# Turned tokens go to their partitions by 4 transfers of 256 KB per group in place of 16 of 64 KB; the turns read features with a step of 4

## The chip, the cores and the metric

The kernel runs on one core of a Trainium2 chip. The metric is the device time of one execution in microseconds. Before the change the median of three runs is 577.77 us (577.75 to 578.08). One further execution was taken with the hardware profiler; all rows quoted below come from it.

The core has a matrix engine (TensorE, in the rows PE; its weight loads have rows of their own, PEld), a vector engine (VectorE, DVE), an activation engine (ScalarE, ACT), a general engine (GpSimd, POOL) and a sync engine (SP) that here only issues transfers. ACT issues some transfers too. Each engine takes its own instructions strictly in order; engines wait for one another by semaphores. Data lies in a memory of 128 partitions (SBUF); products are summed in banks of a second one (PSUM).

## The reference

A conditioned block over x of 2 x 2048 x 512 (f32):

```python
emb = jnp.dot(silu(t), ada_w) + ada_b
shift_msa, scale_msa, gate_msa, shift_mlp, scale_mlp, gate_mlp = jnp.split(emb, 6, axis=-1)
norm = _ln(x) * (1.0 + scale_msa[:, None]) + shift_msa[:, None]
h = gelu(jnp.dot(norm, ssm_w1) + ssm_b1, approximate=False)
x = x + gate_msa[:, None] * (jnp.dot(h, ssm_w2) + ssm_b2)
norm2 = _ln(x) * (1.0 + scale_mlp[:, None]) + shift_mlp[:, None]
hf = gelu(jnp.dot(norm2, ff_w1) + ff_b1, approximate=True)
x = x + gate_mlp[:, None] * (jnp.dot(hf, ff_w2) + ff_b2)
```

`_ln` takes mean and variance over the 512 features. The first two matrices are 512 x 512, the third is 512 x 1024, the fourth 1024 x 512.

## The kernel before

The 4096 tokens are cut into 8 blocks of 512. In a block, partition p holds the four tokens 4p to 4p+3 as four rows c of 512 features. Each block passes through four matrix products, called in the rows by their outputs: hA (first layer), oA (second, added to x), hC (third), oC (fourth, added to x). A matrix product is cut into quarters and done by seven products of quarters, P1 to P7, in place of eight; the sums of quarters that this needs are made on DVE and POOL, and the seven results are added up partly in PSUM and partly by DVE (lines 831 to 851, 886, 934, 1001, 1052, 1098, 1151). The third layer of blocks 1 to 7 goes further: 26 products over a list of registers (`HK_P`), with sums on POOL (L1206) and reads of PSUM by ACT (L1297) and DVE (L1300). Before a product may begin again in a PSUM bank, the DVE or ACT read of what stood there must be over; so a late DVE read can hold PE up.

The order of the work on each engine is written out by hand. A pass over a product takes a table `hooks`: after product "P5", or after round "1b" of a cut product, or after step 17 of the 26, the operations hung there are issued. So an operation of the norm of a later block stands at a fixed place between the DVE reads of the product that PE is busy with.

The change lies in `Norm`. A norm makes statistics (L602, L603, L655 to L704), normalizes four rows c (`normal`, L719 on ACT), and must then turn the block, since a product needs features on the partitions and tokens along them. The turn goes in two steps:

- `turn(c)`, L730: DVE's STREAM_TRANSPOSE turns all 32 x 32 squares of row c, 128 x 512 numbers, from `nT` (or `x`, where the norm is made in place) into the tile `blocks`. There is one buffer of `blocks`.
- `move`, L739: transfers carry the turned squares to the partitions where they belong, back into `nT`. `Q` is 32 and `C` is 4. For each a (source partitions 32a to 32a+31) and each m (destination partitions 32m to 32m+31) there is one transfer of 32 partitions x 2 KB, 16 for a block's norm. With two engines in `engs`, even m go to SP and odd m to ACT.

Then `moved` (`modulate`, L767 on ACT, L769 on DVE) scales and shifts each feature by the block's conditioning, and sums and products follow.

A block's two norms are called `n1[i]` (before hA) and `n2[i]` (before hC). Block 0's first norm is turned by PE (L746). The other 15 use `turn` and `move`: 60 turns and 240 transfers. The turns of `n1[1]`, `n2[0]`, `n1[2]` and `n2[1]` hang in the passes of the first two blocks' hA, oA and hC, before 93 us. The turns of `n1[3]` to `n1[7]` and of `n2[7]` hang in the passes of the 26 products (L1300 between them); the turns of `n2[2]` to `n2[6]` hang in the passes of oC (`residual_in_leaves`, L1052; `residual_in_all_leaves`, L1151). Moves of `n1[1]` and of `n2[2]` to `n2[6]` use SP and ACT; the rest use SP alone, but for `n2[0]`, whose m = 0, 1 are issued by SP in the pass of hA of block 1 and m = 2, 3 by ACT behind that pass.

Of the kernel before, what the change touches and what calls it, by code (L numbers as in the profile page):

```python
# [140 lines left out]
def kernel(  # L141
# [16 lines left out]
    nc = tc.nc  # L158
# [3 lines left out]
    KD = D // P  # L162
    KH = H // P
    C = 4
# [34 lines left out]
    def load_x(i, pieces=1):  # L199
        xs[i] = big_tile(f"x_{i}")  # L200
        for s in range(pieces):
            c = slice(s * C // pieces, (s + 1) * C // pieces)
            nc.sync.dma_start(out=xs[i][:, c, :], in_=x_blk[i][:, c, :])
# [22 lines left out]
    def load_row(t, row):  # L226
        nc.sync.dma_start(out=t, in_=row.unsqueeze(0).to_broadcast([P, D]))
        return t
# [130 lines left out]
    def store_gates(g):  # L359

        to = gates_dram[g].rearrange("b (n m q) -> m b n q", n=KD, q=G)
        for m in range(P // G):
            rows_m = gate_rows[g][m * G : m * G + B, :].rearrange("p (n q) -> p n q", n=KD)
            nc.sync.dma_start(out=to[m], in_=rows_m)

    def load_gate(g, b):

        t = work.tile([P, D], F32, tag=f"gb{g}", name=f"gsb_{g}_{b}", bufs=1)
        gate_rows[g, b] = load_row(t, gates_dram[g][b])
# [143 lines left out]
    Q = P // C  # L513
# [69 lines left out]
    def hook(hooks, places, ops):  # L583

        for n, op in enumerate(ops):
            hooks.setdefault(places[min(n, len(places) - 1)], []).append(op)


    class Norm:
# [136 lines left out]
        def turn(self, c):  # L726

            if c == 0:
                self.bl = self.blocks()
            nc.vector.transpose(  # L730
                self.bl[:, :, :, c, :].rearrange("p m k q -> p k m q"),
                self.nT[:, c, :].rearrange("p (k m q) -> p k m q", k=KD, m=C),
            )

        def move(self, engs=(nc.sync,), part=range(C)):

            for a in range(C):
                for m in part:
                    engs[m % len(engs)].dma_start(  # L739
                        out=self.nT[m * Q : (m + 1) * Q, a, :],  # L740
                        in_=self.bl[a * Q : (a + 1) * Q, m].rearrange("p k c q -> p (k c q)"),
                    )

        def transpose(self, c, pts, first):
            for k in range(KD):
# [713 lines left out]
    hooks = {}  # L1459
# [21 lines left out]
    hooks = {}  # L1481
# [7 lines left out]
    n2 = {0: Norm(0, 2)}  # L1489
# [20 lines left out]
    hooks = {}  # L1510
# [4 lines left out]
    hook(hooks, ("P5", "P7"), fw1_sums[1:3])  # L1515
    hook(hooks, ("P6",), [lambda: gate_rows_of(5)])
    hook(hooks, ("P6", "P7", "P7", "P7"), [lambda c=c: n2[0].turn(c) for c in range(C)])
    hook(hooks, ("P7",), [lambda: n2[0].move((nc.sync,), (0, 1)), lambda: store_gates(5), lambda: load_gate(5, 0), lambda: store_gates(2)])
    load_x(2)
    hA[1] = First(1, n1[1].ops, hooks, FIRST)  # L1520

    n2[0].move((nc.scalar,), (2, 3))
    hA_sums = hA[1].summed(nc.vector)
    run(hA_sums[:2])
    n1[2] = Norm(2, 1)
# [1 line left out]
    hooks = {}  # L1529
# [14 lines left out]
    hooks = {}  # L1544
# [25 lines left out]
    hooks = {}  # L1570
# [10 lines left out]
    hooks = {}  # L1581
# [7 lines left out]
    hooks = {}  # L1589
# [28 lines left out]
    for i in range(1, NBLK):  # L1618
# [4 lines left out]
        hooks = {}  # L1623
        if i == 1:
            assert not fa_sums
        if i == 1:
            engs = dict.fromkeys(("P23", "P4"), nc.gpsimd) | dict.fromkeys(("P5", "P7", "P1", "P6"), nc.vector)
# [60 lines left out]
        hooks = {}  # L1688
        hC_sums = hC.summed(1, nc.vector if alone else nc.gpsimd)
        hook(hooks, EARLY, hC_sums)  # L1690
        engs = (nc.vector if alone else nc.gpsimd, nc.gpsimd, nc.gpsimd)
# [13 lines left out]
        if nx2:  # L1705
# [26 lines left out]
            if ahead:  # L1732
                hooks = {}
# [10 lines left out]
        hooks = {}  # L1744
# [107 lines left out]
        hooks = {}  # L1852
# [81 lines left out]
```

## Time and profile before

| | us |
|---|---|
| median of three runs | 577.77 |
| the profiled execution | 577.74 |
| its span, first to last instruction | 575.9 |
| PE busy | 570.8 (3443 instructions) |
| DVE busy | 453.6 (963) |
| POOL busy | 436.7 (460) |
| ACT busy | 292.7 (574) |

The granted TensorE clock is 1.0 over the execution. A row of the waits reads: engine, tile and line that waited, what ended the wait, sum in us, times, longest. A row of the groups reads: line, engine, operation, out<-in, shapes, count, then busy us and mean ns of one, then idle time of the engine just before them and what ended most of it. A row of the timeline reads: start us, length us (from the first start to the last end where xN instructions are merged), engine, line, operation, and in brackets the idle time before it. PEld stands for the weight load with which a matmul begins; where a matmul must wait, its weight load waits.

### The profile page before, as it was taken

How to read it: one execution, taken by the hardware profiler on the slowest of the kernel's cores; microseconds unless marked ns; L12 is line 12 of the kernel's file. 1: busy time of each engine (PE TensorE's matmuls, PEld its weight loads, DVE VectorE, ACT ScalarE, POOL GpSimd, SP SyncE). 2: the span in 40 equal slices, each digit the busy share in tenths (PEclk: the TensorE clock that was granted, in tenths of full speed). 3: DMA queues.
4: the chain of work that ended last, by engine and by line, in shares of the span. 5: the costliest groups of instructions: out<-in, count | busy, mean ns of one | idle time of the engine just before them, and what ended most of it. 6: DMA issues, size and time to landing. Idle time of an engine off the chain costs nothing.

```text
span 575.9 us, 10119 instructions
## 1 busy us (share of the span) xinstructions
PE 570.8 (99%) x3443; PEld 514.1 (89%) x3443; DVE 453.6 (79%) x963; ACT 292.7 (51%) x574; POOL 436.7 (76%) x460
## 2 busy tenths in 40 slices
PE   8999999999999999999999999999999999999997
PEld 4888888888899889998899988998889999899897
DVE  4968898996878586987869877996768598897676
ACT  3727457705652875448734588326655431742430
POOL 1665449999949869889898999998994885379361
PEclk9999999999999999999999999999999999999999
DMA  8977333303205223283032930243240240031002
GB/s 329 390 232 249 100 71 92 96 38 146 58 18 162 106 100 69 97 260 126 1 93 50 330 115 21 54 109 122 101 109 2 110 126 23 1 73 74 2 1 73
DMA packets 26863, 62.30 MB, mean 108 GB/s; under 512 B 5136, under 2 KB 6204, under 8 KB 25148
## 3 DMA queue, kind: packets, MB, share of 16 engines
q1 hardware_dynamic: 22784, 55.87, 29.9%
q10 hardware_dynamic: 4028, 5.79, 3.9%
q8 instruction: 27, 0.44, 0.4%
q14 instruction: 24, 0.20, 0.1%
HBM read 35.94 MB, written 9.97 MB: 80 GB/s over the span
## 4 chain that ended last, share of the span: by engine, by line
PE 97%; DMA 2%; SPq 0%; DVE 0%; issue 0%; DVEq 0%
PE px_hC L1283 11%; PE py_hA L565 10%; PE py_hC L1283 8%; PE pv_hC L1283 8%; PE pl_oC_P_y L1038 5%; PE py_oC L990 5%; PE pv_hA L565 5%; PE py_oA L925 5%; PE pl_oC_A_y L1133 4%; PE py_oA L565 4%; PE pl_oC_P_v L1038 3%; PE pl_oC_B_y L1133 3%; PE py_hC L565 2%; PE px_hA L565 2%; PE py_oC L565 2%; PE pl_oA_y L940 2%
## 5 line engine op out<-in xcount | busy, mean ns | idle before, releaser
L656 POOL TENSOR_TENSOR r<-ve,minus_half 128x4 f32<-128x4 f32 x16 | 16.6, 1037 | 57.7 <-DVE ve L655 50.7
L767 ACT ACTIVATE nT<-nT,mod,mod 128x512 f32<-128x512 f32 x32 | 23.4, 803 | 46.2 <-DMA nT<-blocks 16.3
L1206 POOL TENSOR_TENSOR forms<-forms 128x256 f32<-128x256 f32 x56 | 42.5, 759 | 3.8 <-DVE forms L1202 0.4
L1283 PE MATMUL py_hC<-forms,fw 128*128 128x256 f32 x168 | 40.9, 379 | 0.0
L1300 DVE TENSOR_TENSOR hClo<-hClo,py_hC 128x512 f32<-128x512 f32 x42 | 28.5, 683 | 11.6 <-ACT hClo L1297 8.2
L719 ACT ACTIVATE nT<-x,nmr,rstd 128x512 f32<-128x512 f32 x36 | 26.8, 803 | 19.4 <-DVE nmr L704 16.8
L1283 PEld LDWEIGHTS py_hC<-forms,fw 128*128 128x128 f32 x168 | 31.7, 190 | 4.6 <-DVE hClo L1300 0.2
L386 POOL TENSOR_TENSOR hSC<-hClo,hChi 128x512 f32<-128x512 f32 (+1 forms) x16 | 19.2, 1205 | 18.7 <-ACT hChi L1278 17.9
L602 DVE BATCH_NORM_STATS2 st<-x 128x6 f32<-128x512 f32 x42 | 28.4, 675 | 4.9 <-DMA x<-in_x_dram 4.9
L1300 DVE TENSOR_TENSOR hChi<-hChi,pv_hC 128x512 f32<-128x512 f32 x35 | 23.2, 678 | 9.2 <-PE pv_hC L1283 5.0
L1278 ACT ACTIVATE hClo<-hClo,colsT 128x256 f32<-128x256 f32 x56 | 25.3, 498 | 5.0 <-DVE hClo L1300 4.8
L1283 PE MATMUL px_hC<-forms,fw 128*128 128x256 f32 x112 | 27.6, 379 | 0.0
L767 ACT ACTIVATE x<-x,mod 128x512 f32<-128x512 f32 x24 | 17.5, 801 | 18.8 <-DMA x<-blocks 18.8
L386 POOL TENSOR_TENSOR hClo<-hClo 128x512 f32<-128x512 f32 (+1 forms) x23 | 26.5, 1154 | 0.0
L1278 ACT ACTIVATE hChi<-hChi,colsT 128x256 f32<-128x256 f32 x56 | 25.1, 496 | 1.9 <-DVE hChi L1300 1.9
L730 DVE STREAM_TRANSPOSE blocks<-nT 128x512 f32<-128x512 f32 x36 | 24.2, 695 | 1.7 <-ACT nT L719 1.7
L1297 ACT ACTIVATE hChi<-py_hC 128x512 f32<-128x512 f32 x14 | 7.6, 594 | 34.0 <-PE py_hC L1283 14.8
L1297 ACT ACTIVATE hClo<-px_hC 128x512 f32<-128x512 f32 x21 | 12.5, 596 | 22.5 <-PE px_hC L1283 18.9
L1283 PEld LDWEIGHTS px_hC<-forms,fw 128*128 128x128 f32 x112 | 21.3, 190 | 2.9
L565 PE MATMUL py_hA<-x,w 128*128 128x256 f32 x96 | 22.7, 379 | 0.0
L1300 DVE TENSOR_TENSOR hChi<-hChi,px_hC 128x512 f32<-128x512 f32 x28 | 19.1, 682 | 4.3 <-ACT hClo L1297 2.1
L1283 PE MATMUL px_hC<-forms,fw_s 128*128 128x256 f32 x84 | 20.5, 380 | 0.0
(537 smaller groups left out, 1921.9 us busy)
## 6 DMA issues: line engine op xcount, KB each, us to landing
x<-in_x_dram SPq DMA_DIRECT2D x13, 1024.0 KB
out_dram<-x SPq DMA_DIRECT2D x14, 512.0 KB
x<-blocks SPq DMA_DIRECT2D x96, 64.0 KB
nT<-blocks SPq DMA_DIRECT2D x88, 64.0 KB
ada<-in_L_cond_ada_w_dram SPq DMA_DIRECT2D x5, 1024.0 KB
fw<-in_L_cond_ff_w_dram SPq DMA_DIRECT2D x2, 2048.0 KB
nT<-blocks ACTq DMA_DIRECT2D x56, 64.0 KB
w<-in_L_cond_ssm_w_dram SPq DMA_DIRECT2D x2, 1024.0 KB
```

What stands on the lines that cost most here:

```text
L386: eng.tensor_tensor(out[:, r], a[:, r], b[:, r], f)
L565: nc.tensor.matmul(ps[b][j * apart][:, j, :], lhs(p, j, k), rhs(p, j, k), start=(fresh and j * (not apart) == 0 and k == 0), stop=(p in (" ...
L602: nc.vector.bn_stats(st, xs[self.i][:, c, :])
L767: nc.scalar.activation(dst, src, AF.Identity, bias=shift, scale=scale)
L925: nc.tensor.matmul(ps[BANK[p]][:, j, :], hops(p, j, k), wops[p][:, k, :], start=False, stop=(k == KD // 2 - 1), skip_group_check=True,)
L990: yield lambda j=j, k=k: nc.tensor.matmul(ps[BANK[p]][:, j, :], hops(p, j, k), wops[p][:, k, :], start=False, stop=(k == kdim - 1), skip_g ...
L1038: nc.tensor.matmul(t[:, n, :], hops.leaves[p][f][:, k, :], leaf_wops[p][f][:, k, :], start=room not in started, stop=(f in ("P2", "P3", "P ...
L1133: nc.tensor.matmul(rooms[g, b][:, at[p], :], hops.leaves[p][f][:, k, :], leaf_wops[p][f][:, k, :], start=(g, b) not in started, stop=(f in ...
L1206: eng.tensor_tensor(reg[d], reg[a], reg[b], ALU.add if f == "+" else ALU.subtract)
L1278: nc.scalar.activation(h, h, AF.Gelu_apprx_tanh, bias=fb1T[:, m : m + 1])
L1283: nc.tensor.matmul(ps[b][:, j, :], fa[ra][:, j * P : (j + 1) * P], fb[rb].rearrange("p a (c q) -> p c a q", q=Q), start=(fresh and j == 0) ...
L1300: nc.vector.tensor_tensor(dest(d), dest(d), ps[b], op)
```

## The change

```diff
             nc.vector.transpose(
                 self.bl[:, :, :, c, :].rearrange("p m k q -> p k m q"),
-                self.nT[:, c, :].rearrange("p (k m q) -> p k m q", k=KD, m=C),
+                self.nT[:, c, :].rearrange("p (k q m) -> p k m q", k=KD, m=C),
             )
 
-        def move(self, engs=(nc.sync,), part=range(C)):
+        def move(self, engs=(nc.sync,)):
 
             for a in range(C):
-                for m in part:
-                    engs[m % len(engs)].dma_start(
-                        out=self.nT[m * Q : (m + 1) * Q, a, :],
-                        in_=self.bl[a * Q : (a + 1) * Q, m].rearrange("p k c q -> p (k c q)"),
-                    )
+                engs[a % len(engs)].dma_start(
+                    out=self.nT[:, a, :],
+                    in_=self.bl[a * Q : (a + 1) * Q].rearrange("p m k c q -> p (m k c q)"),
+                )
...
-    hook(hooks, ("P7",), [lambda: n2[0].move((nc.sync,), (0, 1)), lambda: store_gates(5), lambda: load_gate(5, 0), lambda: store_gates(2)])
+    hook(hooks, ("P7",), [lambda: n2[0].move((nc.sync,)), lambda: store_gates(5), lambda: load_gate(5, 0), lambda: store_gates(2)])
...
-    n2[0].move((nc.scalar,), (2, 3))
```

Feature f of a row used to be read as f = 128k + 32m + q and is now read as f = 128k + 4q + m; in both, feature f ends on partition f mod 128. A turned square (k, m) used to take 32 neighbouring features and now takes every fourth of 128, so its read goes through a row of `nT` in steps of 4 numbers (16 bytes). Partition 32a + q of `blocks` then holds the features of partitions 4q to 4q+3, which lie next to one another, and one transfer per a carries its 32 partitions x 8 KB to all 128 partitions x 2 KB. A group has 4 transfers of 256 KB: two on SP and two on ACT where two engines are given, four on SP elsewhere, `n2[0]` among these. In the program as built, the order of the instructions on PE, DVE and POOL is the same as before; ACT and SP issue fewer transfers.

## The prediction

> **What bounds the kernel now.** I read the page's first part and its chain of waits, then the waits of the weight loads, then those of ACT.
>
> ```profile
> span 575.9 us, 10119 instructions
> PE 570.8 (99%) x3443; PEld 514.1 (89%) x3443; DVE 453.6 (79%) x963; ACT 292.7 (51%) x574; POOL 436.7 (76%) x460
> ...
> PE 97%; DMA 2%; SPq 0%; DVE 0%; issue 0%; DVEq 0%
> ```
>
> ```profile
> PEld py_hC L1283 <- DVE hClo L1300: 0.2, 1, 0.2
> ```
>
> ```profile
> ACT x L767 <- DMA x<-blocks: 18.8, 3, 7.8
> ```
>
> PE is busy for 570.8 of 575.9 us, and the chain that ends last is PE for 97%; its 2% of DMA is the load at the start. So the time is PE's stream plus 5.1 us. The weight loads wait for other engines only in crumbs, of which the quoted one, on a DVE read, is typical. The moves do make ACT wait, 18.8 us in three places, but these waits lie in ACT's own spare time (51% busy). Hence nothing that the change shortens is on the path; what can count is what it makes longer, if that reaches a DVE read that PE waits for. The profiled execution took 577.74 us, its span 575.9, so 1.8 us lie around the span; the median of the runs shown, 577.77, is the same time.
>
> **The change part by part. First the moves.**
>
> ```profile
> 148.58 10.91 SPq L739 DMA_DIRECT2D x<-blocks  x16
> ```
>
> ```profile
> 161.24 2.93 ACT L767 ACTIVATE x<-x,mod 128x512 f32<-128x512 f32 x4 [6.89 <-DMA x<-blocks]
> ```
>
> ```profile
> 33.78 5.15 ACTq L739 DMA_DIRECT2D nT<-blocks  x8
> ...
> 41.00 1.52 ACT L767 ACTIVATE nT<-nT,mod 128x512 f32<-128x512 f32 x2 [10.42 <-DMA fw_t<-in_L_cond_ada_b_dram]
> ...
> 42.38 0.19 PEld L565 LDWEIGHTS py_hA<-nT,w 128*128 128x128 f32 x1
> ```
>
> On one queue a group of 16 takes 10.91 us to issue, 0.68 each, and its reader on ACT starts at 161.24, 1.75 after the last issue ends (159.49): 12.7 in all. On two queues, eight issues each, the group takes 41.00 - 33.78 = 7.2. Removed are 180 of 240 issues: 136 on SP, 44 on ACT. Four issues cost 4 x 0.68 + 1.75 = 4.5 us if a transfer of 256 KB lands as soon as one of 64 KB; from the other side the same 1 MB has been seen to land in 7.2. I take the middle, 5.9. So a move ends 1 to 3 us sooner on two queues and 5 to 8 sooner on one, and what stands behind the moves on SP (loads of x, gates) is issued sooner as well. All of it lies under PE's stream, so I cost it at nothing. If that cover went, the first point would be 42.38, where PE takes the tokens that ACT and DVE modulate from 41.00 on.
>
> **The turns.** This is the part with a price.
>
> ```profile
> L730 DVE STREAM_TRANSPOSE blocks<-nT 128x512 f32<-128x512 f32 x36 | 24.2, 695 | 1.7 <-ACT nT L719 1.7
> L730 DVE STREAM_TRANSPOSE blocks<-x 128x512 f32<-128x512 f32 x24 | 16.7, 704 | 1.4 <-ACT x L719 1.3
> L329 DVE STREAM_TRANSPOSE pada<-pada 128x128 f32<-128x128 f32 x2 | 0.6, 312 | 0.0
> L1202 DVE TENSOR_TENSOR forms<-copy,forms 128x256 f32<-128x256 f32 x16 | 6.0, 419 | 8.2 <-ACT copy L788 5.5 <-POOL forms L1206 2.7
> L1206 DVE TENSOR_TENSOR fw<-fw 128x256 f32<-128x256 f32 x11 | 9.8, 895 | 0.0
> ```
>
> A turn takes 0.695 us for 512 numbers a partition, the same operation 0.312 for 128: (695 - 312) / 384 = 1.0 ns a number, one number a step. No row shows a DVE read whose neighbours are 16 bytes apart. From below, nothing excludes that it runs at the same step: 0. From above, the worst pace at which DVE is seen to get numbers from SBUF is L1206, 895 ns for 256 with both inputs there, against 419 in L1202, where one input is a copy in PSUM: 1.86 ns a number more, 0.95 us a turn. Between 0 and 0.95 I take a second step for each number, 512 x 1.0 ns = 0.51 us, so a turn of 1.2: it is the smallest whole price a read can have that no longer finds the next number beside the last, and it lies nearer to L1206's pace than to none. I keep 0 and 0.95 for the range.
>
> [...]
>
> A group of four turns then ends 4 x 0.51 = 2.04 us later, and 60 turns put 31 us on DVE (79% to 84%). What reaches PE is, at each place, this lateness less DVE's idle time in between and less the slack between the end of the DVE read and the weight load that needs its bank.
>
> ```profile
> 36.41 0.69 DVE L886 TENSOR_TENSOR x<-py_oA,x 128x512 f32<-128x512 f32 x1 [1.04 <-PE py_oA L565]
> 37.31 0.19 PEld L565 LDWEIGHTS py_oA<-w,forms 128*128 128x128 f32 x1 [0.20 <-issue]
> ...
> 57.99 0.68 DVE L886 TENSOR_TENSOR x<-py_oA,x 128x512 f32<-128x512 f32 x1
> 59.13 0.19 PEld L565 LDWEIGHTS py_oA<-w_s,hSA 128*128 128x128 f32 x1
> ...
> 77.29 0.68 DVE L848 TENSOR_TENSOR hChi<-py_hC,hChi 128x512 f32<-128x512 f32 x1
> 78.35 0.19 PEld L565 LDWEIGHTS py_hC<-nS,fw 128*128 128x128 f32 x1
> ...
> 148.47 0.65 DVE L1300 TENSOR_TENSOR hClo<-hClo,px_hC 128x512 f32<-128x512 f32 x1
> 149.24 0.19 PEld L1283 LDWEIGHTS px_hC<-nT,fw 128*128 128x128 f32 x1
> ```
>
> `n1[1]`: the read ends at 37.10, slack 0.21, idle 1.04: 2.04 - 1.25 = 0.79. `n2[0]`: the read ends at 58.67, slack 0.46: 1.58 (DVE is idle before, but waits there for ACT, which waits for a late DVE). `n1[2]`: ends at 77.97, slack 0.38: 1.66. `n1[3]`: ends at 149.12, slack 0.12: 1.92.
>
> ```profile
> 215.73 0.71 DVE L730 STREAM_TRANSPOSE blocks<-x 128x512 f32<-128x512 f32 x1 [0.22 <-ACT x L719]
> 216.37 0.65 DVE L1300 TENSOR_TENSOR hClo<-hClo,pv_hC 128x512 f32<-128x512 f32 x1
> ```
>
> ```profile
> 216.58 1.70 PEld L1283 LDWEIGHTS pv_hC<-nT,fw 128*128 128x128 f32 x8
> ```
>
> ```profile
> 415.37 0.69 DVE L1300 TENSOR_TENSOR hClo<-hClo,py_hC 128x512 f32<-128x512 f32 x1 [0.47 <-ACT hClo L1297]
> 417.47 0.19 PEld L1283 LDWEIGHTS py_hC<-forms,fw 128*128 128x128 f32 x1 [0.20 <-DVE hClo L1300]
> ```
>
> `n1[4]`: two turns stand before the read that ends at 217.02; the second half of PE's eight needs it at 217.45. 1.02 - 0.22 - 0.43 = 0.37. `n1[5]` and `n1[6]` run in the same order; I take the same: 1.1 for three. `n1[7]`: three turns before a place at which PE waits already, 1.53 - 0.47 = 1.06.
>
> ```profile
> 240.44 1.30 DVE L730 STREAM_TRANSPOSE blocks<-nT 128x512 f32<-128x512 f32 x2
> 242.63 1.28 DVE L730 STREAM_TRANSPOSE blocks<-nT 128x512 f32<-128x512 f32 x2
> 243.84 1.44 DVE L1151 TENSOR_TENSOR x<-pl_oC_B_y,x 128x256 f32<-128x256 f32 x5
> 246.03 0.19 PEld L1133 LDWEIGHTS pl_oC_B_y<-fw_s,hSC 128*128 128x128 f32 x1
> ...
> 311.85 1.45 DVE L1151 TENSOR_TENSOR x<-pl_oC_B_y,x 128x256 f32<-128x256 f32 x5
> 314.05 0.19 PEld L1133 LDWEIGHTS pl_oC_B_y<-fw_s,hSC 128*128 128x128 f32 x1
> ...
> 383.40 0.41 DVE L1052 TENSOR_TENSOR x<-pl_oC_P_y,x 128x256 f32<-128x256 f32 x1
> 383.93 0.19 PEld L1038 LDWEIGHTS pl_oC_P_y<-fw,hChi 128*128 128x128 f32 x1
> ...
> 461.01 1.44 DVE L1151 TENSOR_TENSOR x<-pl_oC_B_y,x 128x256 f32<-128x256 f32 x5
> 463.21 0.19 PEld L1133 LDWEIGHTS pl_oC_B_y<-fw_s,hSC 128*128 128x128 f32 x1
> ```
>
> `n2[3]`, `n2[4]`, `n2[6]`: DVE runs without a gap from the turns on; slack 0.75 each: 3 x 1.29 = 3.9. `n2[5]`: slack 0.12: 1.92. The three groups left, `n2[1]`, `n2[2]` and `n2[7]`, I cost at nothing, since DVE idles behind them before PE needs a read:
>
> ```profile
> 89.12 0.69 DVE L848 TENSOR_TENSOR hChi<-py_hC,hChi 128x512 f32<-128x512 f32 x1 [0.42 <-PE py_hC L565]
> ...
> 174.75 1.08 DVE L1052 TENSOR_TENSOR x<-pl_oC_P_x,x 128x256 f32<-128x256 f32 x3 [0.91 <-PE pl_oC_P_x L1038]
> ```
>
> Uncovered, they would cost up to 2.04 each. Sum: 0.79 + 1.58 + 1.66 + 1.92 + 1.1 + 1.06 + 3.9 + 1.92 = 13.9; 577.74 + 13.9 = 591.6.
>
> **The rivals.**
>
> *The turn keeps its pace (not slower).* DVE turns a number a step from any address. Against it: no row has such a read; for it: the same instruction already writes in runs of 32 numbers to far places at 1.0 ns a number. Then DVE's stream is as before, the moves were hidden anyway, and the time is 577.7. [...] The rival decides if the turn's mean stays under 0.8 us.
>
> *Half a step more (0.25 us, 1.0 a group).* By the same subtractions: 0.54 + 0.62 + 0.88 + 0.28 + 3 x 0.25 + 0.88 = 3.95, so 581.7. It needs a read that hides part of its latency.
>
> *The pace of L1206 (0.95 us, 3.8 a group).* 2.55 + 3.34 + 3.42 + 3.68 + 3 x 1.25 + 2.38 + 3 x 3.05 + 3.68 = 32, so 610. DVE would have to be as starved alone as it is there.
>
> *Large transfers land late.* If four take 12.7 us, as 16 on one queue do, in place of 7.2, `n1[1]` comes 5.5 late; less the 0.6 from the end of ACT's first row (41.00 + 0.8) to 42.38, some 4.9: 582 to 583 with unchanged turns. Against it: the bytes are the same.
>
> *Faster.* The moves let PE's crumbs go. They are 0.2 or 0.3 each and hardly one hangs on a move: at best 577.5.
>
> **How the numbers follow.** Forecast 0.50, half a step 0.12, L1206's pace 0.08, late transfers 0.03: slower 0.73. The unchanged turn 0.24; faster 0.03. I take 0.2% (1.2 us) as what a measurement can tell from no change. The likeliest is 591.6; its own range is 587 to 597, from idle time that I counted twice or missed at the places and the three covered groups. The unchanged case holds too much to leave out, so the range goes from 577.4 to 600, and leaves out L1206's pace and a gain.
>
> **What would show it.** Right: the group of L730 has a mean near 1.2 us; weight loads wait for DVE reads (L1300, L1151, L886, L848, L1052) some 14 us in all; the moves are 60 issues, and ACT waits less for them. Wrong: L730 at 0.7 and PE's idle time unchanged; or L730 at 1.2 and no wait of the weight loads, which would mean that I misjudged the slack; or waits of PE on L767, which would mean late transfers.

## The result, and the profile after

The kernel after takes 591.0 us, median of five runs (590.9 to 591.87), against 577.82 for the kernel before on the same chip (577.75 to 578.08): a ratio of 1.023, with a 95% interval of 1.0218 to 1.0241. That is 13.2 us more. The profiled execution took 591.72 us, 0.7 above the median.

The page of the kernel after, its first part and its chain of waits:

```profile
span 589.9 us, 9805 instructions
PE 573.9 (97%) x3443; PEld 513.2 (87%) x3443; DVE 474.9 (81%) x963; ACT 292.9 (50%) x574; POOL 436.2 (74%) x460
...
PE 67%; DVE 17%; DMA 7%; issue 3%; ACT 3%; SPq 1%; POOL 1%; ACTq 0%; DVEq 0%; POOLq 0%
```

The span is 14.0 us longer. PE's share of the chain fell from 97% to 67%, and DVE holds 17% of it now. PE does the same 3443 products; outside them lie 589.9 - 573.9 = 16.0 us, where there were 5.1. The other 3.1 us are inside PE's recorded busy time: the rows of neighbouring products overlap (0.38 us long, 0.22 apart), and across a wait they no longer do.

The groups of the same kernel (line, engine, operation, shapes, count, then busy us and mean ns):

```profile
L730 DVE STREAM_TRANSPOSE blocks<-nT 128x512 f32<-128x512 f32 x36 | 38.9, 1116 | 1.1 <-ACT nT L719 1.1
L730 DVE STREAM_TRANSPOSE blocks<-x 128x512 f32<-128x512 f32 x24 | 26.9, 1126 | 0.0
```

A turn rose from 0.70 to 1.12 us, by 0.42. The 60 turns are busy for 65.8 us in place of 40.9.

The waits of the kernel after (who waited, for what, sum in us, times, longest):

```profile
ACT nT L766 <- DMA nT<-blocks: 53.3, 6, 14.3
...
PEld pl_oC_B_y L1132 <- DVE x L1150: 2.8, 3, 1.0
...
PEld py_hA L565 <- ACT nT L766: 1.9, 2, 1.7
PEld pv_hC L1282 <- DVE hClo L1299: 1.6, 4, 1.0
...
PEld pl_oC_P_y L1037 <- issue: 1.5, 1, 1.5
PEld px_oA L565 <- ACT hA L854: 1.4, 1, 1.4
...
PEld px_hC L1282 <- DVE hChi L1299: 1.3, 2, 1.1
```

Before, these waits of the weight loads were crumbs of 0.2 or 0.3. Three of the rows name a late read on DVE, two name ACT. The row of L1132 is the plainest case: three waits of about 0.95 us, at `n2[3]`, `n2[4]` and `n2[6]`. (Below `move` the line numbers of the kernel after are 1 to 2 lower: L1151 has become L1150, L767 L766, L1283 L1282.) The timeline of the kernel after at the first of them:

```profile
251.63 2.17 DVE L730 STREAM_TRANSPOSE blocks<-nT 128x512 f32<-128x512 f32 x2
253.73 0.37 DVE L1150 TENSOR_TENSOR x<-pl_oC_B_y,x 128x256 f32<-128x256 f32 x1
...
255.22 0.52 PEld L1132 LDWEIGHTS pl_oC_B_y<-fw_s,hSC 128*128 128x128 f32 x4 [0.94 <-DVE x L1150]
```

Two turns take 2.17 us where they took 1.28, the reads of L1150 begin behind them without a gap, and the load that needs their bank stands for 0.94 us.

To see where the time went I took the start of each weight load in both traces: the difference grows from 0 to 13.65 us, in steps. Every step over 0.14 us from 10 us on, at the time that the load had before:

| place (us, before) | what is late | step, us |
|---|---|---|
| 42.38 | moved tokens of `n1[1]`, ACT | 1.65 |
| 57.40 | `n2[0]` | 1.33 |
| 78.35 | `n1[2]` | 1.24 |
| 148.29 and 149.24 | `n1[3]` | 0.97 + 0.83 |
| 188.96 and 204.58 | moved tokens of `n2[2]` | 1.56 + 0.99 |
| 217.45, 285.46, 353.60 | `n1[4]`, `n1[5]`, `n1[6]` | 0.16 + 0.15 + 0.19 |
| 246.03, 314.05, 463.21 | `n2[3]`, `n2[4]`, `n2[6]` | 1.02 + 1.03 + 0.98 |
| 383.93 | `n2[5]` | 1.38 |
| 417.47 | `n1[7]` | 0.39 |
| 99.07, 324.99, 478.66 | others | 0.17 + 0.38 + 0.39 |

They sum to 14.8; some 1.2 is got back between, most of it in steps of 0.1 right behind a wait. The moved tokens, at 42.38 and behind 188.96, make 4.2 of it, and this I had costed at nothing.

### The profile page after: what moved, and what is told of

Same layout as the page of the kernel before. It is cut to its first block, busy times and chain, and to the rows that moved or that the text cites. A ratio compares the mean times of both kernels' runs of the same rounds, so it can differ in the third digit from the quotient of the medians.

```text
span 589.9 us, 9805 instructions
## 1 busy us (share of the span) xinstructions
PE 573.9 (97%) x3443; PEld 513.2 (87%) x3443; DVE 474.9 (81%) x963; ACT 292.9 (50%) x574; POOL 436.2 (74%) x460
## 4 chain that ended last, share of the span: by engine, by line
PE 67%; DVE 17%; DMA 7%; issue 3%; ACT 3%; SPq 1%; POOL 1%; ACTq 0%; DVEq 0%; POOLq 0%
PE px_hC L1282 9%; PE pv_hC L1282 7%; PE py_hA L565 7%; PE py_hC L1282 7%; DVE blocks L730 6%; DMA nT<-blocks 4%; PE py_oA L924 4%; PE pv_hA L565 4%; PE pl_oC_P_y L1037 3%; PE py_oC L989 3%; PE py_oC L565 2%; DVE x L1150 2%; PE px_hA L565 2%; PE pl_oA_y L939 2%; PE pl_oC_P_v L1037 2%
## 5 line engine op out<-in xcount | busy, mean ns | idle before, releaser
L766 ACT ACTIVATE nT<-nT,mod,mod 128x512 f32<-128x512 f32 x32 | 23.4, 803 | 58.0 <-DMA nT<-blocks 40.7
L1282 PE MATMUL py_hC<-forms,fw 128*128 128x256 f32 x168 | 40.9, 380 | 0.2 <-DVE hClo L1299 0.2
L730 DVE STREAM_TRANSPOSE blocks<-nT 128x512 f32<-128x512 f32 x36 | 38.9, 1116 | 1.1 <-ACT nT L719 1.1
L1299 DVE TENSOR_TENSOR hClo<-hClo,py_hC 128x512 f32<-128x512 f32 x42 | 28.4, 680 | 11.0 <-ACT hClo L1296 7.7
L1282 PEld LDWEIGHTS py_hC<-forms,fw 128*128 128x128 f32 x168 | 31.7, 190 | 5.0 <-DVE hClo L1299 0.6
L386 POOL TENSOR_TENSOR hSC<-hClo,hChi 128x512 f32<-128x512 f32 (+1 forms) x16 | 19.0, 1195 | 20.4 <-ACT hChi L1277 17.9
L1299 DVE TENSOR_TENSOR hChi<-hChi,pv_hC 128x512 f32<-128x512 f32 x35 | 23.2, 680 | 8.6 <-PE pv_hC L1282 4.6
L1282 PE MATMUL px_hC<-forms,fw 128*128 128x256 f32 x112 | 27.6, 379 | 0.0
L730 DVE STREAM_TRANSPOSE blocks<-x 128x512 f32<-128x512 f32 x24 | 26.9, 1126 | 0.0
L386 POOL TENSOR_TENSOR hClo<-hClo 128x512 f32<-128x512 f32 (+1 forms) x23 | 26.6, 1159 | 0.0
L1282 PEld LDWEIGHTS px_hC<-forms,fw 128*128 128x128 f32 x112 | 21.3, 190 | 2.9
L1205 POOL TENSOR_TENSOR forms<-nT 128x256 f32<-128x256 f32 x14 | 10.5, 751 | 16.6 <-ACT nT L766 13.5
L1299 DVE TENSOR_TENSOR hChi<-hChi,px_hC 128x512 f32<-128x512 f32 x28 | 19.1, 681 | 4.3 <-ACT hClo L1296 2.1
```

The source lines that it names most:

```text
L386: eng.tensor_tensor(out[:, r], a[:, r], b[:, r], f)
L730: nc.vector.transpose(self.bl[:, :, :, c, :].rearrange("p m k q -> p k m q"), self.nT[:, c, :].rearrange("p (k q m) -> p k m q", k=KD, m=C),)
L766: nc.scalar.activation(dst, src, AF.Identity, bias=shift, scale=scale)
L1205: eng.tensor_tensor(reg[d], reg[a], reg[b], ALU.add if f == "+" else ALU.subtract)
L1282: nc.tensor.matmul(ps[b][:, j, :], fa[ra][:, j * P : (j + 1) * P], fb[rb].rearrange("p a (c q) -> p c a q", q=Q), start=(fresh and j == 0) ...
L1299: nc.vector.tensor_tensor(dest(d), dest(d), ps[b], op)
```

## The experiments

The theory was: the turns with a step of 4 are the whole loss, through late DVE reads. The main rival was that the large transfers land late and take a part of it.

**The turns alone.** The new turns with 16 transfers per group:

```diff
-                self.nT[:, c, :].rearrange("p (k m q) -> p k m q", k=KD, m=C),
+                self.nT[:, c, :].rearrange("p (k q m) -> p k m q", k=KD, m=C),
...
-                        out=self.nT[m * Q : (m + 1) * Q, a, :],
+                        out=self.nT[m :: C, a, :],
```

> The turns read with a step of 4 as in the change, but each group is still moved by 16 transfers of 64 KB (to every fourth partition). The result is the reference's. If the turns alone make the loss, the time is that of the change, 591. If, as the places at which PE falls behind suggest (42.4, 189.0 and 204.6 us of before, 1.65 + 1.56 + 0.99 = 4.2 us, all behind moved tokens), some of it comes from late transfers, it is 591.0 - 4.2 = 587, and PE no longer waits for ACT's modulation there. L730 stays at 1.12 us in both.

589.43 us (589.2 to 589.92), ratio 1.0201 (1.0186 to 1.0216). Its groups:

```profile
L730 DVE STREAM_TRANSPOSE blocks<-nT 128x512 f32<-128x512 f32 x36 | 38.9, 1120 | 1.2 <-ACT nT L719 1.2
```

So the turns, with transfers of the old size, make 11.6 of the 13.2 us, and the size of the transfers the rest. The step at 42.38 is 0.80 here (1.65 after). There is none at 188.96 and 204.58. Three steps stand here that the kernel after does not have: 0.53 at 71.27, 0.39 at 75.01 and 0.82 at 256.97. So the rest, 1.6 us, is a net of what the large transfers cost and what they spare behind slow turns.

**The transfers alone.** The kernel after with the turn of before, once with its two queues and once with all moves on SP:

```diff
-                self.nT[:, c, :].rearrange("p (k q m) -> p k m q", k=KD, m=C),
+                self.nT[:, c, :].rearrange("p (k m q) -> p k m q", k=KD, m=C),
...
-                engs[a % len(engs)].dma_start(
+                nc.sync.dma_start(
```

The second hunk belongs to the second run alone.

> Four transfers of 256 KB per group as in the change, but the turns read features side by side as before, so the tokens reach the products with their features in another order and the output is not the reference's. If the turns alone make the loss: 577.8. If the transfers take a share: 579 to 582, with PE waiting for tokens behind the groups moved on two queues (the first norm of block 1 and the second of block 2). L730 is back at 0.70 us in both.

> As the run with the moves alone, but every move is issued by SP, none by ACT (features in another order again, output not the reference's). If the transfers of ACT are late because the load that SP issues right behind its own two shares the transfer engines with them, the load now stands behind all four and the time comes back to 577.8 to 578.5. If a transfer of 256 KB is late by itself, it stays where the moves alone are, or rises.

On two queues 578.68 us (578.08 to 580.65), ratio 1.0016 (1.0006 to 1.0025); on one 578.08, ratio 1.0004 (0.9994 to 1.0013). With turns of 0.694 us in both, the large transfers cost 0.9 us on two queues, and on one nothing that can be told. In the traces, the loads come late by 0.47 at 204.58 on two queues and by 0.30 at 42.38 on one. So fewer, larger transfers gain nothing here, and cost on two queues. Two rows of the waits say what a sum of waits on ACT is worth. The kernel before:

```profile
ACT nT L767 <- DMA nT<-blocks: 16.3, 3, 8.4
```

and the transfers alone on one queue:

```profile
ACT nT L766 <- DMA nT<-blocks: 60.4, 8, 11.2
```

This row has 44 us more, and the time is the same. All waits of ACT at this line together fell, from 76.6 to 66.8 us: before, most of them stood under other names, where a DVE read, a load or a product came last. So a row of ACT's waits tells what came last, and not what it cost.

**Which steps cost.** One kernel with another step in the turns of blocks 2 to 6, otherwise the kernel after:

```diff
+            s = {3: 2, 4: 4, 5: 8, 6: 16}.get(self.i, 1)
...
-                self.nT[:, c, :].rearrange("p (k q m) -> p k m q", k=KD, m=C),
+                row.rearrange("p (j q s) -> p j s q", q=Q, s=s),
```

Block 2 takes its squares in another order, but numbers side by side, as the other blocks do.

> The changed kernel with another step in the turns of each block: blocks 0, 1 and 7 side by side, block 2 side by side but with its 32 x 32 squares taken in another order, blocks 3, 4, 5 and 6 with steps of 2, 4, 8 and 16 (features in another order, output not the reference's; only the durations of L730's rows count). If the read pays when no two neighbours lie in one 16-byte piece: 0.70 for side by side, both orders, and for step 2, and one price of 1.12 for 4, 8 and 16. If it pays by distance: it grows from 2 to 16. If it is the cutting of the read into runs that costs: 1.12 for block 2 as well.

One run, 583.65 us. Its turns in place, by line (least, median and most ns, then when): L733 is block 2, L741 a step of 2, L743 of 4, L745 of 8, L747 of 16.

```profile
L733 DVE STREAM_TRANSPOSE blocks<-x x4: 670/682/701, 71.7 to 74.1; 128x512 f32<-128x512 f32 x4
```

```profile
L741 DVE STREAM_TRANSPOSE blocks<-x x4: 695/696/704, 144.0 to 148.8; 128x512 f32<-128x512 f32 x4
```

```profile
L743 DVE STREAM_TRANSPOSE blocks<-x x4: 1127/1138/1145, 215.9 to 221.5; 128x512 f32<-128x512 f32 x4
```

```profile
L745 DVE STREAM_TRANSPOSE blocks<-x x4: 1116/1118/1131, 283.9 to 289.5; 128x512 f32<-128x512 f32 x4
```

```profile
L747 DVE STREAM_TRANSPOSE blocks<-x x4: 1062/1082/1095, 353.4 to 358.9; 128x512 f32<-128x512 f32 x4
```

A step of 2 numbers (8 bytes) took 0.70 us, against 0.68 in block 2. One of 4 (16 bytes) took 1.14, 0.44 more, and 8 and 16 cost no more (1.12 and 1.08). So it is not the cutting into pieces (block 2), and from 16 to 64 bytes the distance did not raise the price. The times are those of the first of the three conditions above; a price that begins at some step between 8 and 16 bytes would give the same rows, and a step of 3 numbers, which might part the two, was not run.

**Whether the place decides.** The same 12 slow turns, 5 us of DVE, once in the groups that I had called covered and once in three that I had called open:

```diff
+            self.apart = self.which == 2 and self.i in (1, 2, 7)
+            order = "p (k q m) -> p k m q" if self.apart else "p (k m q) -> p k m q"
...
-                self.nT[:, c, :].rearrange("p (k m q) -> p k m q", k=KD, m=C),
+                self.nT[:, c, :].rearrange(order, k=KD, m=C),
...
-                        out=self.nT[m * Q : (m + 1) * Q, a, :],
+                        out=self.nT[m :: C, a, :] if self.apart else self.nT[m * Q : (m + 1) * Q, a, :],
```

The second run has (3, 4, 6) in the first line.

> The turns with a step of 4 in n2[1], n2[2] and n2[7] alone, side by side in all other groups; 16 transfers of 64 KB throughout, those of the three groups to every fourth partition. The groups of L730 there go from 0.70 to 1.12 us, so DVE gets 12 x 0.42 = 5.0 us more. Theory (a late read costs only where DVE has no idle time and the bank no slack before PE needs it): PE's loads move by under 0.5 us in all, 577.8 to 578.3. Rival (every us that DVE gets more is paid, whatever its place): 582.8.

> The turns with a step of 4 in n2[3], n2[4] and n2[6] alone; 16 transfers of 64 KB throughout. DVE gets the same 5.0 us more as in the run before. Theory: each group ends 4 x 0.42 = 1.7 us later, less 0.75 of slack: 0.93 each at the three loads at 246, 314 and 463 us, 2.8 in all, 580.6; with the 0.8 that a modulated block came late near 257 us in the run of the turns alone, 581.4. Rival (every us is paid): 582.8, as in the run before. If the three places cost nothing: 577.8.

Covered: 577.76 us (577.68 to 578.7), ratio 0.9999 (0.999 to 1.0008). Open: 581.67 us (581.28 to 582.51), ratio 1.0067 (1.0054 to 1.0081). The covered groups, in the groups and the timeline of the first:

```profile
L732 DVE STREAM_TRANSPOSE blocks<-nT 128x512 f32<-128x512 f32 x36 | 28.9, 831 | 1.2 <-ACT nT L719 1.2
```

```profile
91.36 2.12 DVE L732 STREAM_TRANSPOSE blocks<-nT 128x512 f32<-128x512 f32 x2
```

and the waits of the second:

```profile
PEld pl_oC_B_y L1135 <- DVE x L1153: 2.9, 3, 1.0
...
PEld pl_oA_y L942 <- DVE x L957: 0.3, 1, 0.3
```

(The mean of 831 ns is over 12 turns of 1.12 and 24 of 0.70, near enough.) One set of 12 turns is free, the other costs 3.85 us. Lateness less slack is what is paid, not DVE's time. The three places cost 1.07, 1.03 and 1.00, and 0.42 follows at 478.66, which I had not counted; the 0.8 near 257 us that I had carried over from the run of the turns alone is not there. In the timeline of the second run it comes by way of POOL:

```profile
477.66 1.42 DVE L1204 TENSOR_TENSOR forms<-copy,forms 128x256 f32<-128x256 f32 x4 [0.95 <-POOL forms L1208]
```

The same row in the kernel before:

```profile
473.83 1.42 DVE L1202 TENSOR_TENSOR forms<-copy,forms 128x256 f32<-128x256 f32 x4 [0.24 <-POOL forms L1206]
```

DVE waits longer for POOL's sums, and its reads behind (L957) come late with it.

**What the transfers add.** First the kernel after with all moves on SP (the edit is the second hunk above):

> The kernel after, with all 60 moves on SP's queue, so that no transfer of a move runs beside a load that was issued behind it. Theory (late turns cost 10 to 12 us; the rest of the 13.2 is large transfers on ACT's queue that land late beside a load on SP's): the loads of weights near 189 and 204 us come no later than in the run of the turns alone, 588.5 to 590. Rival (large transfers on one queue come as late behind late turns as on two): 591.0. Further rival (one queue makes them later still, since four then go one after the other): 592 to 593.

589.2 us (588.83 to 589.51), ratio 1.0195 (1.0182 to 1.0209): 1.8 less than after. The steps at 188.96 and 204.58 are gone, the one at 42.38 stays at 1.48. What happens behind 180 us shows in the timelines. The kernel after:

```profile
180.53 2.40 ACTq L738 DMA_DIRECT2D nT<-blocks  x2
180.59 1.19 SPq L738 DMA_DIRECT2D nT<-blocks  x2
181.88 1.54 SPq L203 DMA_DIRECT2D x<-in_x_dram  x1
...
192.69 2.93 ACT L766 ACTIVATE nT<-nT,mod,mod 128x512 f32<-128x512 f32 x4 [14.29 <-DMA nT<-blocks]
```

and before:

```profile
173.68 5.26 SPq L739 DMA_DIRECT2D nT<-blocks  x8
179.04 0.52 SPq L203 DMA_DIRECT2D x<-in_x_dram  x1
...
173.57 5.05 ACTq L739 DMA_DIRECT2D nT<-blocks  x8
180.77 2.93 ACT L767 ACTIVATE nT<-nT,mod,mod 128x512 f32<-128x512 f32 x4 [7.98 <-DVE x L1052]
```

From the first issue to use the group takes 192.69 - 180.53 = 12.2 us. Before it took 7.2 at most, as the row there names a DVE read as last. Before, SP needed 5.3 us for its eight issues, so the load of a block of x (1 MB) went out 5.5 us after the first of them; with two issues it goes out 1.3 us after, while the moves are still under way. One run moves that load alone, to ACT behind the modulation (it goes out at 188.04, when the moves have landed), and leaves the moves on two queues:

```diff
-                hook(hooks, ("P5",), [lambda: load_x(i + 3)])
+                hook(hooks, ("P5",), [lambda: xs.update({4: big_tile("x_4")})])
...
+                hook(hooks, ("R2",), [lambda: nc.scalar.dma_start(out=xs[4], in_=x_blk[4])])
```

(This holds for block 4; the loads of the other blocks stay.)

> The kernel after, with one load moved: the 1 MB of block 4, which SP issues at 181.88 right behind its two moves of n2[2], is issued by ACT behind the four modulations of n2[2] instead; the moves stay on two queues. Theory (the moves of n2[2] land late because this load shares the DMA engines with them): issue to modulation falls from 12.2 to about 7 us, the loads of weights near 196 and 212 us come some 1.6 to 2.5 us sooner, 588.5 to 589.4. Rival (two of the four transfers on ACT's queue are late by themselves): 12 us remain, 591.0. If the load itself then comes too late for the statistics of block 4: over 591.

589.22 us (588.61 to 589.53), ratio 1.0194 (1.018 to 1.0208). Its timeline:

```profile
180.22 2.37 ACTq L738 DMA_DIRECT2D nT<-blocks  x2
187.93 0.81 ACT L766 ACTIVATE nT<-nT,mod,mod 128x512 f32<-128x512 f32 x1 [9.84 <-DMA nT<-blocks]
188.04 0.36 ACTq L1810 DMA_DIRECT2D x<-in_x_dram  x1
```

7.7 us from issue to use, and the two steps of 1.56 and 0.99 are gone. So it was the load that ran beside the moves, not ACT's queue.

**A free step.** A turn with a step of 2, and 8 transfers of 128 KB to 64 partitions each:

```diff
-                self.bl[:, :, :, c, :].rearrange("p m k q -> p k m q"),
-                self.nT[:, c, :].rearrange("p (k q m) -> p k m q", k=KD, m=C),
+                self.bl[:, :, :, c, :].rearrange("p (h r) k q -> p k h r q", r=2),
+                self.nT[:, c, :].rearrange("p (k h q r) -> p k h r q", k=KD, h=2, r=2),
...
-                engs[a % len(engs)].dma_start(
-                    out=self.nT[:, a, :],
-                    in_=self.bl[a * Q : (a + 1) * Q].rearrange("p m k c q -> p (m k c q)"),
-                )
+                for h in range(2):
+                    nc.sync.dma_start(
+                        out=self.nT[2 * Q * h : 2 * Q * (h + 1), a, :],
+                        in_=self.bl[a * Q : (a + 1) * Q, 2 * h : 2 * h + 2].rearrange("p m k c q -> p (m k c q)"),
+                    )
```

> A turn with a step of 2 numbers (8 bytes) and 8 transfers of 128 KB per group, each from 32 partitions of 4 KB to 64 partitions of 2 KB, all on SP; feature 128k + 64h + 2q + r. Theory (two numbers of each 16-byte piece are used one after the other's neighbour, which the run with several steps showed to be free): L730 at 0.70 us, 577.8 to 578.5. Rival (the read with one more level of steps is slower, or the price grows with any step): L730 at 0.9 or more, 582 or more. If the transfers of 128 KB land late on one queue: L730 at 0.70 and 579 to 581.

577.9 us (577.72 to 578.96), ratio 1.0001 (0.9992 to 1.001). Its groups:

```profile
L730 DVE STREAM_TRANSPOSE blocks<-nT 128x512 f32<-128x512 f32 x36 | 24.2, 695 | 1.7 <-ACT nT L719 1.7
L730 DVE STREAM_TRANSPOSE blocks<-x 128x512 f32<-128x512 f32 x24 | 16.7, 704 | 1.4 <-ACT x L719 1.3
```

Half as many transfers as before, in the same time. No version beat the kernel before: its bound is PE's stream (570.8 of 575.9 us), which none of these edits touches.

## Why the prediction was right, and where its terms were off

**The bound and the kind of loss: right.** PE's stream was the bound, a slower turn reached it through late DVE reads, and the loss was the lateness less the slack at each place. The two runs on the place show this by themselves: the same 12 slow turns gave 577.76 us in one and 581.67 in the other.

**The price of a turn: too high.** I took 0.51 us, my estimate between 0 and 0.95, as no row of before has such a read; it is 0.42 (1.12 in place of 0.70). The rule that I took it from, one more step of 1.0 ns for each number, does not hold: the price is 0.42 / 512 = 0.8 ns a number. My reason for it was too wide as well: I charged a read that "no longer finds the next number beside the last", and by these words a step of 2 would pay, which at 0.70 us it does not; one of 4 took 1.14 in the same run. The rival of the unchanged turn fell: a turn takes 1.12 us, and its sign was a mean under 0.8.

**The places: nearly right.** With 0.42 a turn, 1.69 a group, my subtractions give 0.44 + 1.23 + 1.31 + 1.57 + 0.57 + 0.79 + 2.82 + 1.57 = 10.3. The table has 9.7 at these places: `n2[0]` 1.33, `n1[2]` 1.24, `n1[3]` 1.80, `n1[4]` to `n1[6]` 0.50, `n1[7]` 0.39, the three groups 3.03, `n2[5]` 1.38, and `n1[1]` nothing at 37.31, the read that I named. `n1[7]` cost half of its repriced term. The three covered groups were covered as far as DVE's reads go. For `n2[0]` the size came out near, but not by the way that I gave. I named the read of L886 and the load at 59.13; what waits is the load at 57.40. In the kernel after, the turns hold up the read of L850, ACT waits for that read, and the load for ACT:

```profile
59.27 0.63 ACT L851 ACTIVATE hA<-hA 128x512 f32<-128x512 f32 x1 [2.31 <-DVE hA L850]
...
60.31 1.59 PEld L565 LDWEIGHTS px_oA<-w,hA 128*128 128x128 f32 x8 [1.35 <-ACT hA L854]
```

**The moves: costed at nothing, and this failed.** The step that failed is "All of it lies under PE's stream, so I cost it at nothing", with its "a move ends 1 to 3 us sooner on two queues". At `n2[6]` no load follows the moves, and in both kernels they are what the modulation waits for last. Before:

```profile
461.12 5.25 ACTq L739 DMA_DIRECT2D nT<-blocks  x8
...
468.57 2.93 ACT L767 ACTIVATE nT<-nT,mod,mod 128x512 f32<-128x512 f32 x4 [1.56 <-DMA nT<-blocks]
```

and after:

```profile
475.10 1.23 ACTq L738 DMA_DIRECT2D nT<-blocks  x2
...
482.51 2.93 ACT L766 ACTIVATE nT<-nT,mod,mod 128x512 f32<-128x512 f32 x4 [5.55 <-DMA nT<-blocks]
```

From the first issue to use it is 7.45 us before and 7.41 after: no sooner. The 7.2 that I took for two queues was not a time of the moves, as the row at 41.00 names the load of `ada_b` that SP issues behind them. At `n2[2]` the move ended some 5 us later instead (12.2 in place of 7.2), as the load behind it was issued sooner. I had written that what stands behind the moves on SP is issued sooner, and not asked what it collides with. That cost 2.55 us of steps, and 1.8 in the end. So the rival of late transfers, to which I gave 0.03, came true in part, at a place that it did not name. At 42.38, the point that I had named for the case that cover goes, PE waited 1.65 us longer, for the modulation, which was my sign of late transfers:

```profile
43.21 1.52 ACT L766 ACTIVATE nT<-nT,mod 128x512 f32<-128x512 f32 x2 [12.59 <-DMA nT<-blocks]
...
44.08 1.59 PEld L565 LDWEIGHTS py_hA<-nT,w 128*128 128x128 f32 x8 [1.68 <-ACT nT L766]
```

These are rows of the kernel after. Of the 1.65, 0.80 is there with the turns alone. There the modulation waits, as before, for the load of `ada_b` behind the moves, and starts 1.4 us later than before (42.41 against 41.00): the lateness of the turns passes through SP's queue.

```profile
42.41 1.52 ACT L767 ACTIVATE nT<-nT,mod 128x512 f32<-128x512 f32 x2 [11.78 <-DMA fw_t<-in_L_cond_ada_b_dram]
```

The rest comes with the large transfers, on one queue as on two: 8.1 us from 35.06 to 43.21, at most 7.2 before. Its size is not sharp, as the step is 1.20 in the run with the load of block 4 moved, which leaves these transfers as they are. A load of 1 MB goes out sooner here too, 2.5 us behind the first move in place of 5.5. Before:

```profile
39.31 0.54 SPq L209 DMA_DIRECT2D ada<-in_L_cond_ada_w_dram  x1
```

and after:

```profile
37.57 3.16 SPq L209 DMA_DIRECT2D ada<-in_L_cond_ada_w_dram  x1
```

But with all moves on SP it goes out 4.3 us behind, and 1.48 of the step remains. No run moved this load, and the cause stays open. On one queue elsewhere I had the direction right, as `n1[3]` in the timeline of the kernel after shows:

```profile
154.29 4.02 SPq L738 DMA_DIRECT2D x<-blocks  x4
...
161.45 2.93 ACT L766 ACTIVATE x<-x,mod 128x512 f32<-128x512 f32 x4 [1.41 <-DMA x<-blocks]
```

161.45 - 154.29 = 7.2 us in place of 12.7: the upper bound, where I took 5.9. The four issues alone take 4.0 us, 1.0 each, where I had taken 0.68.

So 591.6 and 591.0 agree in part by luck, by two errors that offset: the turns, forecast at 13.9, make 11.6 alone, and the transfers, forecast at nothing, add 1.6.

**What would show it.** The group of L730 and the 60 issues came as said. The waits of weight loads on DVE did not: the rows that name DVE hold 5.7 us of those shown, since a late DVE also makes ACT late (the 1.4 behind L854), and some waits stand under another name: 0.9 under POOL's L386, where DVE's L1299 is what ended last, and 1.5 under "issue" at L1037, where the row of the matmul itself names DVE's L1051, with 1.33. ACT does not wait less under the name of the moves but more, 58.7 us against 35.1 (I had read the row of `x` alone, 18.8). At this line in all it waits as long as before, 77.4 us against 76.6.

## What to carry to other kernels

A new access pattern has its price per instruction (0.42 us a turn here), but what it costs is settled place by place: lateness, less the idle time behind it and the slack of the next thing that the bound engine needs (nothing for 12 such turns in one set of places, 3.85 us in another). Before a layout is chosen for larger transfers, look at the read that makes it: with a step of 8 bytes a turn kept its 0.70 us here, with one of 16 it took 1.12. And when issues are taken out of a queue, ask what now leaves that queue sooner and which transfer it runs beside; here a load of 1 MB did, and the moves beside it took 12.2 us in place of 7.7.

## What was not expected of the hardware

From 16 bytes on, the price of a step did not grow with its length: 1138 ns at 16 bytes, 1118 at 32, 1082 at 64, for turns in place. And a group of four transfers of 256 KB on two queues took 12.2 us from first issue to use with a 1 MB load issued 1.3 us behind it, 7.7 without that load.
